# Local attention with a routed expert layer: the gather moved to the head of a block, two one-hot tiles and the clearing of columns moved to the next block

## The chip, the cores and the metric

The kernel runs on one core of a Trainium2 chip. The metric is the device time of one execution in microseconds (us); lower is better. A core has a matrix engine (PE), a vector engine (DVE), a scalar engine (ACT), a general engine (POOL, GpSimd) and DMA queues. Each engine takes its instructions in the order in which the program gives them, and they wait for one another by semaphores. SP is the engine that here only issues plain DMAs.

## The reference, cut to what matters

The input is 2 sequences of 2048 tokens with 256 features, in float32. The first half is attention in a local window with a residual and a layer norm. The second half, which the change touches, is an expert layer with one expert per token:

```python
x = L0_attn_x                                    # (2, 2048, 256)
x = _layernorm(x + attention(x))                 # eps 1e-5
# expert layer, 8 experts of 256 -> 1024, then a shared 1024 -> 256
idx = argmax(softmax(x @ Wr.T))
inter = sum_e (idx == e) * gelu(x @ W1[e] + b1[e])
y = layernorm(inter @ Wo + bo + x) * gamma + beta    # eps 1e-12
out = _layernorm(x + y)                          # eps 1e-5
```

## The kernel before

**Attention.** The first 32 tiles of 128 tokens go through attention in one long hand-ordered stretch. Each finished row is written to DRAM (`x1_d`), and the router's logits are computed on the way. Attention's last pieces end at about 328 us of the span.

**Blocks.** Tokens are then processed in blocks of 128 rows that belong to one expert. There are 25 full blocks (`NFULL`), 0 to 24, whose rows all belong to one expert, and later blocks for what is left over. Which tokens a block holds is a table of row numbers, `g_idx`. The table for blocks 0 to 8 (`g_idx_a`) is ready before the attention stretch ends, because it uses only the first 16 tiles of tokens. The table for blocks 9 to 24 (`g_idx_b`) is made in block 5 by `table(1)`: 32 matmuls on PE, one for each tile of tokens, that add into one result. Each takes as its weights a one-hot tile (`rows[t]`, `one_hots`, line 856) and as its moving operand a slice of `marks`, which DVE makes in steps of the task "others" (lines 928 to 940). Sixteen of the one-hot tiles are made for the last tokens in blocks 1 to 3.

**What a block does.** `block(b)` is a software pipeline over several blocks at once. Written in the order in which the program emits it:

- block b-1 is finished in steps by `finish_block`: DVE adds the residual to the second layer's result (line 264) and takes its statistics; POOL turns a variance into a reciprocal root by an add and a power (lines 255 and 256, `rs_b`); DVE scales twice (lines 267 and 269) and takes statistics again; POOL makes a second root (`rs_c`); DVE makes `res` (line 274), and POOL scatters it to the output by an indirect DMA (line 276, `out_dram`);
- POOL gathers the rows of block b+3 by an indirect DMA (line 150);
- PE runs the first layer of block b+1 (line 222, 32 matmuls), ACT applies the gelus (line 233);
- POOL makes the two residuals of block b+1 (lines 180 and 182, `xbo` and `xbe`);
- PE transposes the rows of block b+2 (line 188, `turn_in`), which a gather has brought one block before;
- PE runs the second layer of block b (line 242, 16 matmuls).

**Work beside.** The dictionary `beside` hangs small tasks into a block at three places. Place 0 comes after the first step of `finish_block`, place 1 after its statistics for the second root, and place 2 after the scatter and ahead of the second layer. The one-hots on POOL are at place 2, as are `table(1)` in block 5 and the clearing of columns of `late_gT` and `late_xT` (line 1506, shown by the profile as line 1471). The steps of "others" are at places 0 and 1 on DVE.

**Order.** All of this runs under a manual schedule: on each engine the instructions stand exactly as the program emits them, and semaphores are derived from the tiles that are read and written. Gathered rows have four buffers (`f6`), transposed rows and weights three, the second layer's results two banks.

Of the kernel before, what the change touches and what calls it, by code (L numbers as in the profile page):

```python
# [17 lines left out]
P = 128  # L18
# [15 lines left out]
def kernel(  # L34
# [16 lines left out]
    nc = tc.nc  # L51
# [9 lines left out]
    GB = 3  # L61
# [3 lines left out]
    NFULL = -((E * (P - 1) - B * T) // P)  # L65

    ND = NT - NFULL
# [66 lines left out]
    late = {}  # L134
# [5 lines left out]
    def of_block(tables, b, rows=slice(None)):  # L140
        n = 0 if b < NA else 1 if b < NFULL else 2
        at = b - (0, NA, NFULL)[n]
        return tables[n][rows, at : at + 1]

    def gather(b):
        if b < NFULL:
            xg = f6.tile([P, C], F32, tag="xg", name=f"xg_{b}")
        else:
            xg = late["d"].tile([P, C], F32, tag="xd", name=f"xd_{b}")
        nc.gpsimd.indirect_dma_start(  # L150
            out=xg,
            out_offset=None,
            in_=x1_d[0 : (SPLIT[EARLY] * P if b < NA else B * T), :],
            in_offset=bass.IndirectOffsetOnAxis(ap=of_block(g_idx, b), axis=0),
        )
        xgs[b] = xg
# [19 lines left out]
    def residuals(b):  # L176

        pool, n = (late["s"], "") if b < NFULL else (late["d"], "d")
        xbos[b] = pool.tile([P, C], F32, tag=f"xbo{n}", name=f"xbo_{b}")
        nc.gpsimd.tensor_tensor(xbos[b], xgs[b], bo_bc, ALU.add)  # L180
        xbes[b] = xgs[b] if n else pool.tile([P, C], F32, tag="xbe", name=f"xbe_{b}")
        nc.gpsimd.tensor_tensor(xbes[b], xgs[b], be_bc, ALU.add)

    def turn_in(b):
        px = turned(f"pg_{b}")
        px = px.rearrange("p a t -> p (a t)")
        for k in range(KC):
            nc.tensor.transpose(px[:, ts(k, P)], xgs[b][:, ts(k, P)], ident)
        if b < NFULL:
            xT = f3.tile([P, KC, P], F32, tag="xgT", name=f"xgT_{b}")  # L190
        else:
            xT = late["xT"][:, :, ts(b - NFULL, P)]
        xTs[b] = px, xT

    def keep_in(b):
        px, xT = xTs[b]
        nc.scalar.copy(xT, px[:, 0:C].rearrange("p (k t) -> p k t", k=KC))
# [10 lines left out]
    def first_layer(b, units):  # L208

        wb, xT = wbs[b], (picked[b][1] if b in picked else xTs[b][1])  # L210
        for f in units:
            h = f // (NF // 2)
            if f == 0:
                if b < NFULL:
                    gTs[b] = f2.tile([P, NF, P], F32, tag="gT", name=f"gT_{b}")
                banks_of[b] = 2 * (len(banks_of) % 2)
            if f % (NF // 2) == 0:
                phs[b, h] = ps_s.tile(
                    [P, 4, P], F32, tag=f"s{banks_of[b] + h}", name=f"ph_{b}_{h}"
                )  # L220
            for k in range(KC):
                nc.tensor.matmul(  # L222
                    phs[b, h][:, f % (NF // 2), :],
                    lhsT=wb[:, k, ts(f, P)], rhs=xT[:, k, :],
                    start=(k == 0), stop=(k == KC - 1),
                )

    def gelus(b, h):
        ph = phs.pop((b, h))

        gT = late["gT"][:, :, ds(picked[b][0], P)] if b in picked else gTs[b]
        for f in range(h * NF // 2, (h + 1) * NF // 2):
            nc.scalar.activation(  # L233
                gT[:, f, :], ph[:, f % (NF // 2), :], AF.Gelu,
                bias=bcs[b][:, f : f + 1], scale=1.0,
            )
# [11 lines left out]
    def stats(v, eps, name):  # L248

        st = fs.tile([P, 6], F32, tag=f"st{name[0]}", name=f"st_{name}")  # L250
        mv = fs.tile([P, 2], F32, tag=f"mv{name[0]}", name=f"mv_{name}")
        nc.vector.bn_stats(st, v)
        nc.vector.bn_aggr(mv, st)  # L253
        rs = fs.tile([P, 1], F32, tag=f"rs{name[0]}", name=f"rs_{name}")
        nc.gpsimd.tensor_tensor(rs, mv[:, 1:2], eps, ALU.add)  # L255
        nc.gpsimd.tensor_tensor(rs, rs, minus_half, ALU.pow)  # L256
        return mv, rs
# [3 lines left out]
    def finish_block(b, places=s_idx):  # L261

        y = late["3"].tile([P, C], F32, tag="y", name=f"y_{b}")
        nc.vector.tensor_tensor(y, pys.pop(b)[:, 0:C], xbos[b], ALU.add)  # L264
        mv, rs = stats(y, eps_ffn, f"b{b}")
        yield
        nc.vector.scalar_tensor_tensor(y, y, mv[:, 0:1], ga_bc, ALU.subtract, ALU.mult)
        yield
        nc.vector.scalar_tensor_tensor(y, y, rs, xbes[b], ALU.mult, ALU.add)
        yield  # L270
        mv, rs = stats(y, eps_block, f"c{b}")
        yield
        res = late["3"].tile([P, C], F32, tag="res", name=f"res_{b}")
        nc.vector.tensor_scalar(res, y, mv[:, 0:1], rs, ALU.subtract, ALU.mult)  # L274

        ins = nc.gpsimd.indirect_dma_start(  # L276
            out=of[:, :],
            out_offset=bass.IndirectOffsetOnAxis(ap=of_block(places, b), axis=0),
            in_=res,
            in_offset=None,  # L280
            bounds_check=B * T - 1,
            oob_is_err=False,
        )

        if places is s_idx:
            for other in written:
                tc.declare_no_dep(ins.ins, other.ins, reason="other rows")
            written.append(ins)
        yield


    with ExitStack() as att:
# [915 lines left out]
        for i in range(NT):  # L1208


            t, u, w, z = (n if n >= 0 else None for n in range(i, i - 4, -1))
# [127 lines left out]
        tiles = list(range(*lots[lot]))  # L1339
# [85 lines left out]
    def first_done(b):  # L1425

        at = line.index(b) + 3
        if at < len(line):
            load_weights(line[at])

    def block(b):

        last = finish_block(b - 1)
        next(last)
        for task in beside.get((b, 0), ()):
            task()
        if b + 3 < NFULL:
            gather(b + 3)
        if b + 1 < NFULL:
            first_layer(b + 1, range(NF // 2))  # L1440
            gelus(b + 1, 0)
            residuals(b + 1)
        next(last)
        next(last)
        next(last)
        for task in beside.get((b, 1), ()):
            task()
        if b + 1 < NFULL:
            first_layer(b + 1, range(NF // 2, NF))
            gelus(b + 1, 1)  # L1450
            first_done(b + 1)
        if b + 2 < NFULL:
            turn_in(b + 2)
            keep_in(b + 2)
        for n in firsts[b]:
            if n >= NFULL:
                first_layer(n, range(NF))
                gelus(n, 0)
                gelus(n, 1)
                first_done(n)  # L1460
        n = b - begin + 1 + NFULL
        if NFULL <= n < NFULL + ND:
            turn_in(n)
            keep_in(n)
            residuals(n)
        for m in firsts.get(b + 1, ()):
            if m >= NFULL:
                pick(m)
        next(last)
        for task in beside.get((b, 2), ()):  # L1470
            task()
        if begin - 2 <= b < begin - 2 + ND:
            gather(b - begin + 2 + NFULL)
        second_layer(b)
# [5 lines left out]
    beside = {  # L1480
        (1, 0): [partial(rest, ("hot", lot))],
        (1, 2): [partial(rank, lot)] + [partial(one_hots, nc.gpsimd, t) for t in tiles[:4:2]],
        (2, 0): [partial(rest, ("places", lot))],
        (2, 1): [partial(one_hots, nc.vector, t) for t in range(*lots[lot], 2)]
        + [partial(some, "others", 3)],
        (2, 2): [partial(one_hots, nc.gpsimd, t) for t in tiles[4:8:2]],
        (3, 0): [partial(some, "others", 6)],
        (3, 1): [partial(some, "others", 9)],
        (3, 2): [partial(one_hots, nc.gpsimd, t) for t in tiles[8::2]],
        (4, 0): [partial(some, "others", 3)],  # L1490
        (4, 1): [partial(rest, "others")],
        (5, 2): [partial(table, 1)],
        (14, 0): [partial(table, 2)],
    }
# [4 lines left out]
    for b in range(10, 14):  # L1499
        at = 8 * (b - 10)  # L1500
        beside[b, 0] = [partial(late_one_hots, nc.vector, at, at + 3)]
        beside[b, 1] = [partial(late_one_hots, nc.vector, at + 3, at + 8)]
    for b in range(4, 8):

        beside.setdefault((b, 2), []).append(
            partial(nc.gpsimd.memset, late["gT"][:, 2 * b - 8 : 2 * b - 6, (ND - GB) * P :], 0.0)
        )
    beside[8, 2] = [partial(nc.gpsimd.memset, late["xT"][:, :, ND * P :], 0.0)]

    def close(blocks, places):  # L1510

# [17 lines left out]
    for b in range(1, NFULL):  # L1529
        block(b)  # L1530
# [48 lines left out]
```

## Time and profile before

| | us |
|---|---|
| three runs | 584.72, 583.76, 584.75 |
| median | 584.72 |
| the profiled execution's own time | 584.71 |
| its span in the trace | 582.9 |
| time around the span | 1.8 |

| engine | busy us | share |
|---|---|---|
| PE | 555.4 | 95% |
| POOL | 409.1 | 70% |
| DVE | 397.2 | 68% |
| ACT | 302.0 | 52% |

The span is one execution as the trace shows it, from its first to its last instruction. Shares are means over stages with different limits, so for a change in one stage the timeline of that stage is what has to be read: for each engine the start of an instruction, its duration, what it is, and in brackets the idle time ahead of it with what ended that. Several of the same kind in a row are merged in one line (`x16`).

### The profile page before, as it was taken

To read this page: it belongs to the slowest core of one execution; us is meant where nothing else is said; L and a number is where in the kernel's file an instruction comes from. 1 tells how busy PE (TensorE), PEld (TensorE's weight loads), DVE (VectorE), ACT (ScalarE), POOL (GpSimd) and SP (SyncE) were. 2 spreads that over 40 slices of the span, in tenths; PEclk is the share of its full clock that TensorE was granted. 3 is DMA by queue.
4 is the path that set the end of the run, shared out by engine and by line. 5 is a ranking of instruction groups with operands and counts; after the bars stand their busy time and mean duration, and the time that the engine had idled before them with its cause. 6 is when DMAs were issued, how large, how long until landed. Compare 5 with 4: busy or idle time off the path is not lost. (4 is left out here: it accounts for less than half of the span.)

```text
span 582.9 us, 18515 instructions
## 1 busy us (share of the span) xinstructions
PE 555.4 (95%) x7311; PEld 452.4 (78%) x7312; DVE 397.2 (68%) x966; ACT 302.0 (52%) x1005; POOL 409.1 (70%) x603
## 2 busy tenths in 40 slices
PE   8999999999999999999898999999999999999991
PEld 5658667676776766766667899899999999999980
DVE  5559788887888788889977467887864242242483
ACT  2487675766758576675755433233334445545200
POOL 5359777676777877878983388888788767642484
PEclk9999999999999999999999999999999999999997
DMA  5301603012031120201343455555555766754010
GB/s 163 86 2 46 178 24 98 21 45 78 12 88 37 46 76 12 62 25 30 109 115 118 173 178 172 180 185 186 182 177 191 249 202 232 240 191 154 19 39 28
DMA packets 35605, 64.79 MB, mean 111 GB/s; under 512 B 8558, under 2 KB 23484, under 8 KB 35516
## 3 DMA queue, kind: packets, MB, share of 16 engines
q1 hardware_dynamic: 32444, 55.19, 30.2%
q0 software_dynamic: 3072, 8.39, 4.5%
q8 instruction: 59, 0.97, 0.7%
q14 instruction: 30, 0.25, 0.1%
HBM read 48.93 MB, written 8.39 MB: 98 GB/s over the span
## 5 line engine op out<-in xcount | busy, mean ns | idle before, releaser
L561 ACT ACTIVATE pr<-s,nm 128x128 f32<-128x128 f32 x512 | 142.1, 412 | 3.8 <-DVE nm L557 3.7
L573 POOL TENSOR_TENSOR fd<-pr 128x512 f32<-128x512 f32 x62 | 79.0, 1274 | 65.6 <-ACT pr L561 65.6
L233 ACT ACTIVATE gT<-ph,bc 128x128 f32<-128x128 f32 x200 | 57.2, 370 | 107.4 <-issue 60.4
L222 PEld LDWEIGHTS ph<-xgT,wb 128*128 128x128 f32 x800 | 93.5, 192 | 1.3
L222 PE MATMUL ph<-xgT,wb 128*128 128x128 f32 x800 | 94.4, 275 | 0.0
L242 PE MATMUL py<-wo_sb,gT 128*128 128x256 f32 x400 | 90.6, 380 | 0.0
L557 DVE TENSOR_REDUCE nm<-s 128x4 f32<-128x512 f32 x128 | 82.4, 683 | 5.9 <-PE s L545 5.5
L581 POOL TENSOR_TENSOR fd<-fd 128x512 f32<-128x512 f32 (+2 forms) x93 | 76.6, 824 | 7.3
L242 PEld LDWEIGHTS py<-wo_sb,gT 128*128 128x128 f32 x400 | 74.1, 190 | 9.0
L622 ACT COPY pT<-pt 128x512 f32<-128x512 f32 x64 | 38.3, 599 | 70.0 <-DVE nm L557 39.3
L616 PE MATMUL pt<-ident,pr 128*128 128x128 f32 x512 | 71.4, 280 | 1.8 <-ACT pT L622 0.6
L616 PEld LDWEIGHTS pt<-ident,pr 128*128 128x128 f32 x512 | 55.5, 141 | 18.2 <-issue 9.6
L426 PE MATMUL pj<-xT,wa 128*128 128x512 f32 x128 | 60.6, 595 | 0.8 <-issue 0.8
L264 DVE TENSOR_TENSOR y<-py,xbo 128x256 f32<-128x256 f32 x32 | 13.5, 422 | 52.9 <-PE py L242 52.8
L624 DVE COPY pT<-pt 128x512 f32<-128x512 f32 x64 | 43.8, 684 | 7.8 <-PE pt L616 7.8
L545 PEld LDWEIGHTS s<-k,q 32*64 32x64 f32 x2048 | 30.9, 130 | 15.0 <-issue 15.0
L222 PE MATMUL ph<-xpT,wb 128*128 128x128 f32 x352 | 40.8, 275 | 0.0
L222 PEld LDWEIGHTS ph<-xpT,wb 128*128 128x128 f32 x352 | 40.1, 192 | 0.1
L545 PE MATMUL s<-k,q 32*64 32x128 f32 x2048 | 38.6, 278 | 0.0
L426 PEld LDWEIGHTS pj<-xT,wa 128*128 128x128 f32 x128 | 21.7, 190 | 17.6 <-issue 15.5
L274 DVE TENSOR_SCALAR res<-y,mv_c,rs_c 128x256 f32<-128x256 f32 x32 | 15.9, 498 | 28.4 <-POOL rs_c L256 23.4
L255 POOL TENSOR_TENSOR rs_b<-mv_b,eps_ffn 128x1 f32<-128x1 f32 x32 | 9.3, 291 | 36.8 <-DVE mv_b L253 31.1
(235 smaller groups left out, 999.2 us busy)
## 6 DMA issues: line engine op xcount, KB each, us to landing
wb<-in_L_ffn_W_dram SPq DMA_DIRECT2D x33, 1024.0 KB
h<-v SPq DMA_DIRECT2D x24, 192.0 KB, 3.7
xt<-in_L_attn_x_dram SPq DMA_DIRECT2D x8, 512.0 KB, 4.0
x_d<-x SPq DMA_DIRECT2D x32, 128.0 KB, 1.8
wb<-in_L_ffn_W_dram SPq DMA_DIRECT2D x24, 128.0 KB, 2.1
h<-v SPq DMA_DIRECT2D x14, 96.0 KB, 2.7
wo_sb<-in_L_ffn_Wo_dram SPq DMA_DIRECT2D x1, 1024.0 KB
wa<-in_L_attn_W_attn_dram SPq DMA_DIRECT2D x3, 256.0 KB, 5.1
```

Source lines behind the costliest of these rows:

```text
L222: nc.tensor.matmul(phs[b, h][:, f % (NF // 2), :], lhsT=wb[:, k, ts(f, P)], rhs=xT[:, k, :], start=(k == 0), stop=(k == KC - 1),)
L233: nc.scalar.activation(gT[:, f, :], ph[:, f % (NF // 2), :], AF.Gelu, bias=bcs[b][:, f : f + 1], scale=1.0,)
L242: nc.tensor.matmul(py[:, 0:C], lhsT=gT[:, f, :], rhs=wo_sb[:, f, :], start=(f == 0), stop=(f == NF - 1),)
L426: nc.tensor.matmul(pm, lhsT=wa[:, k, ts(f, P)], rhs=axT[c][:, k, :], start=(k == 0), stop=(k == KC - 1),)
L545: nc.tensor.matmul(banks[i][r][a * CTX : (a + 1) * CTX, 2 * g + o, :], lhsT=qs[c][rows, g, o, t0 : t0 + CTX], rhs=ks[c][rows, g, t0 : t0 + P],
L557: nc.vector.tensor_reduce(maxes[i][:, r, :], banks[i][r], AX.X, ALU.max, negate=True)
L561: nc.scalar.activation(probs[i][:, r, x, :], banks[i][r][:, x, :], AF.Exp, bias=maxes[i][:, r, x : x + 1], scale=1.0,)
L573: nc.gpsimd.tensor_tensor(fd[:, 8 * pair : 8 * pair + 8, :], pr[:, two, :, 0:CTX].rearrange("p r x c -> p (r x) c"), pr[:, two, :, CTX:P]. ...
L581: nc.gpsimd.tensor_tensor(fd[:, :, 0:n], fd[:, :, 0:n], fd[:, :, n : 2 * n], ALU.add)
L616: nc.tensor.transpose(pt[:, x, :], probs[i][:, r, x, :], ident)
L622: nc.scalar.copy(pTs[i][:, r], pt)
L624: nc.vector.tensor_copy(pTs[i][:, r], pt)
```

## The change

Three moves in the order of the program; no arithmetic is changed.

1. In `block(b)`, the gather of block b+3 is emitted first of all, ahead of the first step of `finish_block(b - 1)`. Before, it came after that step and after the tasks at place 0.
2. Of the four one-hot tiles that POOL made at place 2 of block 3 (tokens' tiles 24 to 27), two (26 and 27) are made at place 2 of block 4.
3. The clearing of columns is moved by a block: `late_gT` from blocks 4 to 7 to blocks 5 to 8, `late_xT` from block 8 to block 9.

```diff
     def block(b):
 
+        if b + 3 < NFULL:
+            gather(b + 3)
         last = finish_block(b - 1)
         next(last)
         for task in beside.get((b, 0), ()):
             task()
-        if b + 3 < NFULL:
-            gather(b + 3)
         if b + 1 < NFULL:
             first_layer(b + 1, range(NF // 2))
...
-        (3, 2): [partial(one_hots, nc.gpsimd, t) for t in tiles[8::2]],
+        (3, 2): [partial(one_hots, nc.gpsimd, t) for t in tiles[8:10:2]],
         (4, 0): [partial(some, "others", 3)],
         (4, 1): [partial(rest, "others")],
+        (4, 2): [partial(one_hots, nc.gpsimd, t) for t in tiles[10::2]],
         (5, 2): [partial(table, 1)],
...
-    for b in range(4, 8):
+    for b in range(5, 9):
 
         beside.setdefault((b, 2), []).append(
-            partial(nc.gpsimd.memset, late["gT"][:, 2 * b - 8 : 2 * b - 6, (ND - GB) * P :], 0.0)
+            partial(nc.gpsimd.memset, late["gT"][:, 2 * b - 10 : 2 * b - 8, (ND - GB) * P :], 0.0)
         )
-    beside[8, 2] = [partial(nc.gpsimd.memset, late["xT"][:, :, ND * P :], 0.0)]
+    beside[9, 2] = [partial(nc.gpsimd.memset, late["xT"][:, :, ND * P :], 0.0)]
```

## The prediction

> **What bounds the kernel now.** I read PE's timeline from the start of the block stage first, because PE has the largest busy share (95%).
>
> ```profile
> 353.44 3.73 PE L222 MATMUL ph<-xgT,wb 128*128 128x128 f32 x32
> 357.01 0.38 PE L188 MATMUL pg<-ident,xg 128*128 128x128 f32 x2
> 357.23 3.62 PE L242 MATMUL py<-wo_sb,gT 128*128 128x256 f32 x16
> 360.68 3.73 PE L222 MATMUL ph<-xgT,wb 128*128 128x128 f32 x32
> 365.30 0.41 PE L188 MATMUL pg<-ident,xg 128*128 128x128 f32 x2 [0.88 <-DMA xg<-x_d,g_idx_a]
> 365.54 0.95 PE L951 MATMUL p_tok<-marks,row 128*128 128x32 bf16 x32
> 366.35 3.70 PE L242 MATMUL py<-wo_sb,gT 128*128 128x256 f32 x16
> 369.88 3.73 PE L222 MATMUL ph<-xgT,wb 128*128 128x128 f32 x32
> ```
>
> A block takes PE 7.24 us (353.44 to 360.68), back to back. Block 5 is the exception: its transposes (L188) come 4.62 us after the first layer's start, not 3.57 as in block 4. PE waits 1.05 us for the gather of block 7. After that PE is full again, so any time that PE loses or wins here reaches the end of the span. Two smaller holes of the same kind follow: first layers start 7.36 us apart around 380 and 7.50 around 395, 0.11 and 0.26 too long.
>
> Next I read why that gather was late, in POOL's timeline for blocks 3 and 4.
>
> ```profile
> 357.38 1.04 POOL L276 DMA_INDIRECT out_dram<-res,g_idx_a  x1 [1.14 <-DVE res L274]
> 358.46 2.56 POOL L856 TENSOR_SCALAR row<-col,lows 128x128 bf16<-128x128 f32 x4
> 361.00 0.18 POOL L255 TENSOR_TENSOR rs_b<-mv_b,eps_ffn 128x1 f32<-128x1 f32 x1
> 361.26 0.57 POOL L256 TENSOR_TENSOR rs_b<-rs_b,minus_half 128x1 f32<-128x1 f32 x1
> 362.02 1.31 POOL L150 DMA_INDIRECT xg<-x_d,g_idx_a  x1 [0.19 <-issue]
> 363.37 0.81 POOL L180 TENSOR_TENSOR xbo<-xg,bo_bc 128x256 f32<-128x256 f32 x1
> 364.14 0.89 POOL L182 TENSOR_TENSOR xbe<-xg,be_bc 128x256 f32<-128x256 f32 x1
> 365.00 0.23 POOL L255 TENSOR_TENSOR rs_c<-mv_c,eps_block 128x1 f32<-128x1 f32 x1
> 365.31 0.60 POOL L256 TENSOR_TENSOR rs_c<-rs_c,minus_half 128x1 f32<-128x1 f32 x1
> 366.65 1.04 POOL L276 DMA_INDIRECT out_dram<-res,g_idx_a  x1 [0.74 <-DVE res L274]
> ```
>
> POOL's gathers start 9.48, 9.06 and 9.40 us apart in blocks 1 to 4 (334.08, 343.56, 352.62, 362.02): it is over 7.24, so POOL falls behind PE. The gather of 362.02 frees PE at 365.30, 3.28 us after its start. POOL is also idle 1.14 us ahead of the scatter, for DVE's `res`; so I read DVE's turn in the same loop.
>
> ```profile
> 353.96 0.79 DVE L1011 TENSOR_TENSOR base<-first_of,taken 128x8 f32<-128x8 f32 x1
> 356.68 0.41 DVE L274 TENSOR_SCALAR res<-y,mv_c,rs_c 128x256 f32<-128x256 f32 x1
> 361.87 0.49 DVE L269 SCALAR_TENSOR_TENSOR y<-y,rs_b,xbe 128x256 f32<-128x256 f32 x1 [1.89 <-POOL rs_b L256]
> 365.95 0.41 DVE L274 TENSOR_SCALAR res<-y,mv_c,rs_c 128x256 f32<-128x256 f32 x1 [0.28 <-POOL rs_c L256]
> ```
>
> So there is a ring: POOL's `rs_b` frees DVE's L269; L269, statistics and the tasks at place 1 lead to `res`; `res` frees the scatter; then come the one-hots, and then `rs_b` of the next block. From L269 to `res` DVE takes 4.21 us in block 3 (352.47 to 356.68), 3.86 in block 2, 4.08 in block 4. The gather and the residuals stand beside this DVE time, so the gather's 1.31 us costs the ring nothing now.
>
> **The change part by part.** *The gather goes ahead of `rs_b`.* In block 1 it falls into POOL's idle 5.53 us ahead of 333.03 and is free: the residuals start 1.3 us earlier, and `res` follows `rs_c` about 0.93 us earlier. From block 2 on it stands in the ring: 0.18 gap + 1.31 + 0.04 = 1.53 us ahead of `rs_b`, on which L269 waits, then everything behind L269 on DVE, then the scatter. It is the wait that this change adds.
>
> *What DVE does then.* In before the place-1 tasks run beside `xbo` and `xbe`, and tiny ones are slow there: L1011 took 0.79 us on 128x8 beside `xbo`, L1047 0.17 on the same shape with POOL on a single-column operation. The Trainium skill (GPSIMD Engine Reference, section 1, Specifications) says that POOL shares SBUF interfaces with DVE, and that DVE instructions with two SBUF inputs are among those that contend. This trace agrees, and the rule speaks for a smaller loss: with the gather gone from between, `xbo` and `xbe` start at L269 and end at about L269 + 1.4, just after the tasks begin (L269 + 1.08). Without contention block 3's tasks would take about 2.0 us for 3.2, but L269 itself would suffer (0.76 for 0.48 where it met the gather's end and `xbo` at 431 us). By the unchanged rows D, from L269 to `res`, is 3.86, 4.21 and 3.75 (4.08 without 0.28 of waiting) in blocks 2, 3, 4; without contention about 3.3 each. I take 3.45, 3.50, 3.45, nearer to the freed case, as POOL does only single-column work beside most tasks.
>
> *The ring, worked out.* L269 comes 0.87 us after `rs_b`; the scatter 0.70 after `res`; 1.08 later POOL is free; one-hots are 0.645 each (2.58 for four).
> - Block 1: POOL ends at 342.53 - 0.93 = 341.60.
> - Block 2: `rs_b` 343.13, L269 344.00, `res` 347.45, scatter 348.15, end 348.15 + 1.08 + 2.58 = 351.81 (before 351.60).
> - Block 3: `rs_b` 353.34, L269 354.21, `res` 357.71, scatter 358.41, end with two one-hots 360.78.
> - Block 4: gather of block 7 at 360.96 (before 362.02), lands by the same 3.28 at 364.24; PE wants it at 364.25. The 1.05 us hole goes. Then `rs_b` 362.31, L269 363.18, `res` 366.63, scatter 367.33, and only then the two moved one-hots, done at 367.33 + 1.08 + 1.29 = 369.70.
>
> *The moved one-hots have a reader.* `table(1)` in block 5 reads `rows[26]` and `rows[27]`; PE reaches it at about 364.5. In before these tiles were done at 361.0 and hidden; now PE, in order, waits for 369.70. Some six matmuls of the table's 32 remain (0.95 us for 32): 0.2. The second layer starts at 369.9; before at 366.35. PE loses 3.55 us. What is behind it, second layer and first layer of block 7, waits with it.
>
> *The clearing.* Four memsets of 0.98 and one of 0.34 leave blocks 4 to 8 and enter 5 to 9. Block 4 is 0.98 lighter, which is already in the sum (none after its scatter); the columns are first read past 436 us, so there is no reader to be late for.
>
> *After block 5.* The late PE gives gathers slack: gather 8 starts at 369.88, lands some 4.15 later (376.70 to 380.79 and 391.22 to 395.53 in before say 4.1 to 4.3), and is wanted at 369.9 + 3.46 + 3.57 = 376.9: 2.9 us of slack. The holes of 0.11 and 0.26 go: -0.37. But the ring with a memset is 1.53 + 0.87 + D + 0.70 + 1.06 + 0.98 = 5.14 + D; with D reduced as above to 2.75, 3.1, 2.85, 3.1 in blocks 5 to 8 (unchanged rows 3.16, 3.75, 3.16, 3.34) it loses 0.64 + 0.99 + 0.74 + 0.99 = 3.36 against PE's 7.25: about 0.45 more than the slack, a hole at the transposes of block 12 near 400 us. Block 9 has the small memset and 2.2 of DVE; blocks 10 to 13 with no memset are at 7.0; no more is lost. From 16 on PE has 11 us per block and POOL catches up.
>
> *DMA and queues.* The same gathers, scatters and loads are issued. SP's queue has no step moved. On POOL's own queue the gather is now right behind the scatter (about 1 us after its end, 2 before); if it landed 0.5 us later, slack takes it in blocks 5 to 7.
>
> *The clock.* PE's idle stretch in block 5 is about 5 us in all. The trace has the price of a cold PE at its start: 16 transposes took 3.67 us, 229 ns each, where 32 matmuls of that size now take 3.73, 0.12 us each. The Trainium skill (TensorE: Matmul & The Clock Gate, section "What's actually happening") puts the fall to half rate after an idle window of about 3.4 us, and as long to recover. By the rows of before (PEclk 9 through holes to 1.24 us) I add nothing; by the rule it would be an estimated +1.7 us. I take nothing: PE is busy with the table's first 16 matmuls, waits for `marks` (to about 366.3), does 10 more, and waits again for 3.3 us, so no stretch quite fills a window. It stays in the upper range.
>
> Sum: 3.55 - 0.37 + 0.45 = +3.6 on the profiled execution's 584.71 (582.9 span and 1.8 around it; the median 584.72 is the same): **588.3 us**.
>
> **The rivals.** *Contention stays (slower still).* With D unchanged the same ring gives one-hots at 371.1, second layer 371.3, so +4.95, and holes of some 1.5 us near 395 and 403: +6.1, 590.8. For it: POOL's `xbo` still meets two-input DVE work. Against: tasks are clear of it.
>
> *Only the one-hots count (no change).* If the gather did not delay `rs_b`, block 4's L269 would come at 361.87 - 1.29 = 360.58, `res` 364.4, one-hots 367.5, second layer 367.7: +1.35 - 0.37 = +1.0, 585.7. Against it: POOL's next instruction starts 0.04 us after every gather's end.
>
> *The gather was the only thing in the way (faster).* Mechanism: PE's 1.05 us hole at the transposes in block 5 goes, with 0.37 later, and nothing replaces it: 583.3. It decides at the table: the one-hots must be done by about 365.1, so the scatter of block 4 has to be out at 362.7, some 3.9 us earlier than the 366.65 of before. Nothing in the change takes this much from POOL and DVE ahead of it.
>
> **How the numbers follow.** My forecast, a table that waits 3 to 5 us, has 0.70; contention kept, or a cold clock on top, 0.20; only the one-hots 0.05; faster 0.05. The forecast's own ends are the freed D (+2.4) and the middle of both D (+4.1) with a hole or two: 586.6 to 590. The range 586.4 to 590.7 leaves out the two last cases and half of the second. A change of 0.2%, 1.2 us, is about what can be told from none: faster 0.05, same 0.05, slower 0.90.
>
> **What would show it.** In PE's timeline: the transposes of block 5 at 364.3 without a wait; the table's matmuls split, the rest after POOL's one-hots at 368.5 to 371; the second layer at 369 to 371. In POOL's: gather, `rs_b`, residuals in this order, DVE's L269 of blocks 3 and 4 1.3 to 2.4 us later than before. Wrong would be: a table that runs at 364.5 to 366 in one piece; L269 no later; or matmuls of the first layer after it at twice their duration (the clock).

## The result and the profile after

| | us |
|---|---|
| before, median of 4 runs | 584.27 (583.76 to 584.75) |
| after, median of 4 runs | 588.66 (588.41 to 589.87) |
| ratio | 1.0081, 95% interval 1.0069 to 1.0094 |
| span of the profiled execution, before and after | 582.9, 586.7 |
| forecast | 588.3, range 586.4 to 590.7 |

The change makes the kernel 4.4 us slower, clear of noise. Everything is lost in one place, block 5. PE's timeline after the change, the part that answers to the one shown of before (start, duration, what, idle time before and its end):

```profile
360.38 3.73 PE L222 MATMUL ph<-xgT,wb 128*128 128x128 f32 x32
363.95 0.38 PE L188 MATMUL pg<-ident,xg 128*128 128x128 f32 x2
364.17 0.56 PE L951 MATMUL p_tok<-marks,row 128*128 128x32 bf16 x16
365.38 0.40 PE L951 MATMUL p_tok<-marks,row 128*128 128x32 bf16 x10 [0.65 <-DVE marks L940]
368.21 0.19 PE L951 MATMUL p_tok<-marks,row 128*128 128x32 bf16 x1 [2.43 <-POOL row L856]
368.80 0.32 PE L951 MATMUL p_tok<-marks,row 128*128 128x32 bf16 x5 [0.40 <-POOL row L856]
368.96 5.19 PE L242 MATMUL py<-wo_sb,gT 128*128 128x256 f32 x16
373.98 3.73 PE L222 MATMUL ph<-xgT,wb 128*128 128x128 f32 x32
```

The transposes (L188) no longer wait for the gather: they come 3.57 us after the first layer's start, as in block 4. The table (L951) now waits three times: for DVE's marks (0.65 us), and for each of the two moved one-hots (2.43 and 0.40). The second layer behind it takes 5.19 us where it took 3.70. From one first layer to the next, block 5 takes 13.60 us (360.38 to 373.98) against 9.20 before: +4.40. The holes of 0.11 and 0.26 us that before had near 380 and 395 are gone (-0.37). That is +4.03, and the block stage began 0.30 us earlier in this execution, so PE ends 3.73 later; the spans differ by 3.8.

Why the table waits is in POOL's timeline of blocks 3 and 4 after the change:

```profile
358.09 1.04 POOL L276 DMA_INDIRECT out_dram<-res,g_idx_a  x1 [1.55 <-DVE res L274]
359.18 1.32 POOL L856 TENSOR_SCALAR row<-col,lows 128x128 bf16<-128x128 f32 x2
360.67 1.06 POOL L150 DMA_INDIRECT xg<-x_d,g_idx_a  x1 [0.17 <-PE py L242]
361.76 0.20 POOL L255 TENSOR_TENSOR rs_b<-mv_b,eps_ffn 128x1 f32<-128x1 f32 x1
...
362.60 0.72 POOL L180 TENSOR_TENSOR xbo<-xg,bo_bc 128x256 f32<-128x256 f32 x1
...
366.42 1.05 POOL L276 DMA_INDIRECT out_dram<-res,g_idx_a  x1 [0.96 <-DVE res L274]
367.53 1.22 POOL L856 TENSOR_SCALAR row<-col,lows 128x128 bf16<-128x128 f32 x2
```

The gather of block 7 starts at 360.67, not 362.02, and that is what removed PE's hole. But the two one-hots stand behind block 4's scatter, which stands behind DVE's `res`, and run at 367.5 to 368.8; PE was at the table at 364.2.

DVE in the same stretch, the other half of the ring:

```profile
354.01 0.96 DVE L269 SCALAR_TENSOR_TENSOR y<-y,rs_b,xbe 128x256 f32<-128x256 f32 x1 [3.20 <-POOL rs_b L256]
355.73 0.20 DVE L1011 TENSOR_TENSOR base<-first_of,taken 128x8 f32<-128x8 f32 x1
357.39 0.41 DVE L274 TENSOR_SCALAR res<-y,mv_c,rs_c 128x256 f32<-128x256 f32 x1
362.65 0.96 DVE L269 SCALAR_TENSOR_TENSOR y<-y,rs_b,xbe 128x256 f32<-128x256 f32 x1 [2.11 <-POOL rs_b L256]
365.72 0.41 DVE L274 TENSOR_SCALAR res<-y,mv_c,rs_c 128x256 f32<-128x256 f32 x1
```

L269 waits longer for `rs_b` than before (3.20 us in block 3), as the gather is now ahead of `rs_b`. It also takes twice as long, 0.96 for 0.48 us, since POOL's `xbo` and `xbe` now run beside it; the tasks behind it have become short (L1011 0.20 for 0.79).

The clock, by stretches of PE's time in the changed kernel (columns: stretch, its length, busy time of PE, PEld, DVE, ACT and POOL with counts, granted clock, DMA share, GB/s):

```profile
364.00:366.00 2.00, 1.12 (x29) 0.93 (x27) 1.86 (x9) 1.41 (x5) 1.22 (x3) 1.00 0.43 33
366.00:369.00 3.00, 0.39 (x7) 0.30 (x7) 2.75 (x9) 0.00 (x0) 2.36 (x4) 0.93 0.97 373
369.00:371.00 2.00, 2.00 (x10) 1.64 (x7) 0.10 (x1) 0.00 (x0) 1.90 (x4) 0.50 0.17 41
371.00:372.50 1.50, 1.50 (x7) 1.22 (x6) 1.43 (x4) 0.00 (x0) 1.43 (x2) 0.67 0.09 33
372.50:374.00 1.50, 1.50 (x9) 1.32 (x8) 1.23 (x10) 0.00 (x0) 0.74 (x2) 1.00 0.00 0
```

Read in finer stretches of the same view, PE was granted half its clock from 368.57 to 371.98, 3.41 us that begin in the last short wait and lie almost wholly in the second layer. So the wait is paid twice: as idle time, and in the matmuls after it. Below, *cold* stands for half clock and *warm* for the full one.

### The profile page after: what moved, and what is told of

Read it like the earlier page. It is cut to its first block, busy times and chain, and to the rows that moved or that the text cites. A ratio compares the mean times of both kernels' runs of the same rounds, so it can differ in the third digit from the quotient of the medians.

```text
span 586.7 us, 18516 instructions
## 1 busy us (share of the span) xinstructions
PE 556.6 (95%) x7311; PEld 453.5 (77%) x7312; DVE 392.2 (67%) x966; ACT 301.9 (51%) x1005; POOL 407.0 (69%) x603
## 5 line engine op out<-in xcount | busy, mean ns | idle before, releaser
L242 PE MATMUL py<-wo_sb,gT 128*128 128x256 f32 x400 | 92.1, 384 | 0.0
L269 DVE SCALAR_TENSOR_TENSOR y<-y,rs_b,xbe 128x256 f32<-128x256 f32 x25 | 22.5, 899 | 31.6 <-POOL rs_b L256 31.4
L667 PE MATMUL py<-wpj,av 128*128 128x256 f32 x128 | 34.0, 388 | 1.0 <-ACT x1T L710 0.4
```

Of the source, the lines that this page charges most:

```text
L242: nc.tensor.matmul(py[:, 0:C], lhsT=gT[:, f, :], rhs=wo_sb[:, f, :], start=(f == 0), stop=(f == NF - 1),)
```

## The experiments

The theory is this: the early gather mends PE's hole but lengthens the ring of POOL and DVE; the two moved one-hots have a reader on PE that comes first; and the wait costs clock on top. The rivals: the gather's move is free, or the one-hots alone account for everything.

**Gather alone.** Only the first move is made.

```diff
     def block(b):
+        if b + 3 < NFULL:
+            gather(b + 3)
         last = finish_block(b - 1)
         next(last)
...
-        if b + 3 < NFULL:
-            gather(b + 3)
```

> Only the gather is moved to the head of the block; the one-hots and the clearing stay where they were before. My theory (the gather stands in the ring POOL rs_b, DVE L269 to res, POOL scatter): L269 of blocks 3 and 4 later than before as in the changed kernel, the gather of block 7 starts at about 362 because all four one-hots are ahead of it, so PE keeps a hole of about 1.3 us at the transposes of block 5; the table then waits for DVE's marks until about 366.6 but not for POOL; no cold matmuls. Second layer of block 5 some 1 us later than before, and a few tenths more from later holes: about 585.6, +1.3 us. Rival (the early gather is free and only the moved one-hots cost time): the hole of 1.05 us shrinks, 583.3 to 584.3.

Measured: 587.42 us against 584.71 of before in the same series, ratio 1.0045 (1.0032 to 1.0059). The gather's move is no gain by itself: the rival falls. Block 5 went as worked out, +0.94 us (10.14 for 9.20), with a gather at 362.18, hardly other than before, and a wait for DVE's marks. But 1.8 us came in two places that I had not expected. PE's timeline of this kernel in blocks 5 and 14:

```profile
365.21 0.41 PE L188 MATMUL pg<-ident,xg 128*128 128x128 f32 x2 [0.79 <-DMA xg<-x_d,g_idx_a]
366.88 0.55 PE L951 MATMUL p_tok<-marks,row 128*128 128x32 bf16 x16 [0.87 <-DVE marks L940]
...
428.89 0.83 PE L951 MATMUL p_tok<-marks,late_row 128*128 128x14 bf16 x27
430.26 0.96 PE L951 MATMUL p_tok<-marks,late_row 128*128 128x14 bf16 x5 [0.54 <-DVE late_row L862]
```

The second table, in block 14, waits for the last five one-hots that DVE makes behind L269 in block 13; from the first layer ahead of this table to the one behind it 9.49 us pass, 8.05 before. As I read the timelines, DVE is late since the ring is slower than PE through blocks 5 to 8 (gathers 7.34 to 7.94 us apart, where PE takes 7.24). The other hole is in block 15, in its transposes of the leftover rows: 7.80 us to the next first layer, 7.47 before. In the changed kernel PE is itself 4 us late by then, and neither hole shows.

**All but the gather.** One-hots and clearing are moved, the gather is not.

```diff
     def block(b):
-        if b + 3 < NFULL:
-            gather(b + 3)
         last = finish_block(b - 1)
         next(last)
...
+        if b + 3 < NFULL:
+            gather(b + 3)
```

> The one-hots and the clearing are moved as in the change, the gather stays behind rs_b. My theory: the hole at the transposes of block 5 goes, as the gather of block 7 starts 1.3 us earlier; L269 of block 4 at about 360.6, res 364.4, scatter 365.1, the two moved one-hots done at 367.4, so the table waits on POOL some 2.4 us and the second layer of block 5 starts 1.2 us later than before; later holes (0.37 us) gone: +0.9 us, 585.1, with a warm clock; with a cold second layer as in the changed kernel up to 586.6. Rival (the gather's move costs nothing, all of the loss is the moved one-hots): the same 588.6 as the changed kernel.

Measured: 587.36, ratio 1.0043 (1.0029 to 1.0056), +2.65 us. PE's timeline in block 5:

```profile
364.19 0.81 PE L951 MATMUL p_tok<-marks,row 128*128 128x32 bf16 x26
366.97 0.19 PE L951 MATMUL p_tok<-marks,row 128*128 128x32 bf16 x1 [1.97 <-POOL row L856]
367.55 0.29 PE L951 MATMUL p_tok<-marks,row 128*128 128x32 bf16 x5 [0.39 <-POOL row L856]
367.68 5.39 PE L242 MATMUL py<-wo_sb,gT 128*128 128x256 f32 x16
```

The second layer starts 1.3 us later than before (1.2 expected), and then runs cold although the long gap is under 2 us: 5.39 for 3.70 us. Block 5 takes 12.51 us for 9.20, of which 1.62 is the wait and 1.69 the clock; the mended holes (0.37) and a block stage that began 0.28 earlier in this execution bring that to the 2.65. The rival (all of the changed kernel's loss) falls too. The two parts, +2.7 and +2.65, make +4.4 together and not 5.4, as the late PE hides the gather's holes in blocks 14 and 15.

**One-hots early in block 4.** The whole change, with the two one-hots behind `rs_b`.

```diff
-        (4, 0): [partial(some, "others", 3)],
+        (4, 0): [partial(some, "others", 3)]
+        + [partial(one_hots, nc.gpsimd, t) for t in tiles[10::2]],
...
-        (4, 2): [partial(one_hots, nc.gpsimd, t) for t in tiles[10::2]],
```

> The whole change, but the two moved one-hots come in block 4 right behind rs_b and ahead of the residuals, not behind the scatter. My theory: they are done at about 364, the table waits only for DVE's marks (to about 365.5), the second layer of block 5 starts about 365.8, 0.3 us earlier than before, matmuls stay at full clock; the ring with the memset (7.4 us a block, PE 7.25) makes small holes in blocks 6 to 10 of about 0.7 us in all where before had 0.37: 584.3, no change against before, 4.3 us under the changed kernel. Rival (the loss is the gather's delay of the ring, the one-hots only mark it): the time stays within 1.5 us of the changed kernel, 587 to 588.6.

Measured: 586.14, ratio 1.0024 (1.0015 to 1.0033), +1.43 where I expected none; but nearly 3 us under the changed kernel's loss, which settles that the place of these two tiles makes most of it. The miss is in two terms. The residuals, pushed back, now met the marks on DVE, whose first operation took 0.95 us, not 0.39; PE's table waited for them until 365.87:

```profile
362.54 0.61 DVE L269 SCALAR_TENSOR_TENSOR y<-y,rs_b,xbe 128x256 f32<-128x256 f32 x1 [2.11 <-POOL rs_b L256]
363.75 0.95 DVE L928 TENSOR_TENSOR same<-label,at 128x256 f32<-128x256 f32 x1
364.73 0.83 DVE L935 TENSOR_TENSOR marks<-same,tile 128x256 bf16<-128x256 f32 x1
```

And block 14's table had the hole of "Gather alone" again, 8.93 us for 8.05, with 0.26 in block 15.

**A filled wait.** The whole change with 28 transposes of the identity ahead of the table, whose result nobody reads.

```diff
+    def fill(count):
+        pf = turned("fill")
+        for _ in range(count):
+            nc.tensor.transpose(pf[:, 0, :], ident, ident)
...
-        (5, 2): [partial(table, 1)],
+        (5, 2): [partial(fill, 28), partial(table, 1)],
```

> The whole change with 28 extra transposes of the identity on PE ahead of the table in block 5, which nobody reads; they fill some 3.1 us in which PE would wait for the one-hots. My theory (the wait makes the clock fall, and the next second layer pays 1.56 us for it): the one-hots are done at the same time, the second layer of block 5 starts within 0.2 us of the changed kernel's, but takes 3.6 us and not 5.2: 587.1, 1.6 us under the changed kernel. Rival (the slow 16 matmuls have another cause, such as late weights or gelus): no change, 588.6.

Measured: 587.62, +2.91 against before in its series, where the change has +4.39: 1.5 us back by adding work.

```profile
364.40 3.22 PE L1484 MATMUL fill<-ident 128*128 128x128 f32 x28
367.46 0.80 PE L951 MATMUL p_tok<-marks,row 128*128 128x32 bf16 x26
368.56 0.19 PE L951 MATMUL p_tok<-marks,row 128*128 128x32 bf16 x1 [0.29 <-POOL row L856]
369.40 0.29 PE L951 MATMUL p_tok<-marks,row 128*128 128x32 bf16 x5 [0.65 <-POOL row L856]
369.54 3.70 PE L242 MATMUL py<-wo_sb,gT 128*128 128x256 f32 x16
```

The second layer is back at 3.70 us. It starts 8.92 us after block 5's first layer (8.58 in the changed kernel), behind the same one-hots, so the slow matmuls came from idle PE time and from nothing in the data. The mean granted clock was 0.991 to 0.993 in all five executions, as in 14 of the 15 of before in that series; the changed kernel's four have 0.986 to 0.989.

**How long a wait may be.** 18 and 8 transposes in the same place, one execution each.

> The changed kernel with 18 extra transposes (read by nobody) ahead of the table in block 5, so that PE's wait for the first moved one-hot is about 1.3 us, in place of the 2.43 us of the changed kernel and the 0.29 us with 28 of them. My theory (it is one long gap that lets the clock fall; 1.1 us did not, 1.97 us did): the second layer of block 5 takes 3.6 to 3.7 us, clock 1.00 throughout. Rival (it is the busy share over some microseconds that counts, and tiny table matmuls hardly count): 5.2 us, as in the changed kernel.

> The same with 8 extra transposes: the wait for the first moved one-hot is about 2.3 us, but the idle time before it, for DVE's marks, is filled. My theory (one gap over some 2 us is enough): second layer of block 5 in 5.2 us, clock half for about 3.4 us. Rival (the sum of the idle time counts, and it is about 0.8 us less than in the changed kernel): 3.7 us.

Both expectations were wrong, and the wrong way round: with 18 (gaps of 1.31 and 0.66 us) the second layer took 5.39 us, total 588.51; with 8 (gaps of 0.40, 1.92 and 0.66) it took 3.70, total 586.95. The first execution with 18:

```profile
367.87 0.19 PE L951 MATMUL p_tok<-marks,row 128*128 128x32 bf16 x1 [1.31 <-POOL row L856]
368.72 0.29 PE L951 MATMUL p_tok<-marks,row 128*128 128x32 bf16 x5 [0.66 <-POOL row L856]
368.86 5.39 PE L242 MATMUL py<-wo_sb,gT 128*128 128x256 f32 x16
```

So neither a longest gap nor the sum of the idle time decides. The same two kernels over more executions:

> The kernel with 18 extra transposes once more, now timed over many executions. It showed a cold second layer after a gap of 1.31 us, where 8 transposes and a gap of 1.92 us left it warm. If the clock is decided by a window that runs on its own time, an execution falls in it by chance: times spread over two groups some 1.7 us apart, near 586.9 and 588.5. If the program alone decides (which matmuls fill the time), all executions are near 588.5 with the spread of the kernel before.

> The kernel with 8 extra transposes, timed over many executions. By a window on its own time: two groups, near 586.9 and 588.5. If the program alone decides: all near 586.9.

In the profiled executions of these the two had changed sides: 18 transposes, same gap, warm (first three lines); 8 transposes, a gap of 1.84, cold (last three).

```profile
368.28 0.19 PE L951 MATMUL p_tok<-marks,row 128*128 128x32 bf16 x1 [1.31 <-POOL row L856]
369.11 0.29 PE L951 MATMUL p_tok<-marks,row 128*128 128x32 bf16 x5 [0.65 <-POOL row L856]
369.25 3.70 PE L242 MATMUL py<-wo_sb,gT 128*128 128x256 f32 x16
...
369.02 0.19 PE L951 MATMUL p_tok<-marks,row 128*128 128x32 bf16 x1 [1.84 <-POOL row L856]
369.87 0.31 PE L951 MATMUL p_tok<-marks,row 128*128 128x32 bf16 x5 [0.66 <-POOL row L856]
370.02 6.62 PE L242 MATMUL py<-wo_sb,gT 128*128 128x256 f32 x16
```

Times were 587.97 to 590.07 with 18 (median 589.30, before 584.43), and 588.71 to 590.91 with 8 (median 589.46): no two clean groups near 586.9 and 588.5, and some slower than either, so this part of the expectation did not come. What is shown is that the same program at the same gap is warm in one execution and cold in another.

The traces also show what tells the two apart. The clock switched only at points that lie whole multiples of 3.413 us apart: in the changed kernel it fell at 368.57, rose at 371.98, and fell again, behind PE's last work, at 576.78, which is 60 times 3.413 us later. So the points in block 5 can be found from an execution's later switches even where the clock stayed up. PE's busy time in the emptiest stretch of block 5 between two such points, and the clock behind it:

| profiled execution | stretch, us | PE busy, us | clock behind it |
|---|---|---|---|
| changed kernel | 365.16 to 368.57 | 0.59 (17%) | half for 3.41 us |
| 8 transposes, second | 365.70 to 369.12 | 1.19 (35%) | half for 6.83 us |
| all but the gather | 365.19 to 368.60 | 1.24 (36%) | half for 3.41 us |
| 18 transposes, first | 366.30 to 369.71 | 1.44 (42%) | half for 3.41 us |
| 18 transposes, second | 367.32 to 370.73 | 1.81 (53%) | full |
| 8 transposes, first | 367.14 to 370.55 | 1.89 (55%) | full |
| gather alone | 364.77 to 368.19 | 2.11 (62%) | full |
| before | 362.73 to 366.15 | 2.54 (74%) | full |

In block 5 the clock fell after 42% or less and held after 53% or more (with the one-hots early after 68%, with 28 transposes after 72%). Where the points lie against PE's waits differs from one execution to the next, and with gaps like these that decides. It is no rule for every mix of matmuls: in the profile of the next experiment the clock fell at 35.87 us, in attention, after a stretch of 64%. With 8 transposes the second profile was cold for two stretches, the first of which holds the gap of 0.66 us; the second layer then took 6.46 us to the next first layer, 2.9 more than warm. With a block stage that began 1.1 us later than in the first, this makes its 590.91.

The Trainium skill (TensorE: Matmul & The Clock Gate, section "What's actually happening") gives the gate's window as 3413 ns and calls it free-running, not reset when a kernel starts; the switch points agree. It puts the fall to half rate after an idle window of about 3.4 us. Here gaps of 1.31 and 0.66 us, with the table's tiny matmuls around them, were enough when the points lay badly, and the measurement decides.

**Residuals later.** The whole change with `residuals(b + 1)` moved behind `rs_c`.

```diff
-            residuals(b + 1)
         next(last)
         next(last)
         next(last)
+        if b + 1 < NFULL:
+            residuals(b + 1)
```

> The whole change, with POOL's two residuals of a block moved behind rs_c, so that they no longer run beside DVE's L269 but beside the place-1 tasks. My theory (POOL and DVE slow each other whenever a POOL elementwise operation meets DVE work on two inputs, so contention moves and does not go): L269 takes 0.48 us and not 0.95, but the marks operations of block 4 take 0.6 to 0.9 us as in before, not 0.4; res of block 4 within 0.4 us of the changed kernel's 365.7, one-hots done at 368.5 to 369.2; 588.0 to 589.2. Rival (only L269 suffers, the tasks are slow in before for another reason): L269 0.48 and the tasks stay short, each block's ring is 0.47 us shorter, the one-hots are done 1.2 us earlier, 587.2 to 587.5.

Measured: 590.47, ratio 1.0108 (1.0093 to 1.0124): 1.7 us worse than the change, where I had at most 0.5. L269 was free again (0.48 us), and the marks stayed short as well (0.39, 0.42, 0.35), which the theory had not foreseen: POOL now idles 1.28 us for DVE's statistics and starts the residuals after the marks. They hit what came next, `res`:

```profile
363.97 0.48 DVE L269 SCALAR_TENSOR_TENSOR y<-y,rs_b,xbe 128x256 f32<-128x256 f32 x1 [2.12 <-POOL rs_b L256]
365.48 0.42 DVE L935 TENSOR_TENSOR marks<-same,tile 128x256 bf16<-128x256 f32 x1
366.48 0.58 DVE L1019 TENSOR_TENSOR taken<-taken,first_of 128x8 f32<-128x8 f32 x1
366.99 0.88 DVE L274 TENSOR_SCALAR res<-y,mv_c,rs_c 128x256 f32<-128x256 f32 x1
```

This execution runs 1.26 us behind the changed kernel's from before the first block (the cold stretch at 35.87 us lies there), so `res` at 366.99 is the 365.72 from there, no better, and it takes 0.88 us for 0.41. The moved one-hots come 0.47 us later for it, and block 5 takes 14.12 us, 0.52 more than in the changed kernel. The ring is not shortened by moving the contention: the second half of the theory stands, the rival falls. The rest of the 1.7 us is a new hole of 1.10 us in block 15, where PE waits for a leftover gather.

**Six one-hots in POOL's idle time.** Ahead of block 1 POOL is idle 5.5 us, and the columns that one-hots are made from are ready. Six of the twelve go there, and two each into blocks 1, 2 and 3; once on the kernel before, once on the changed kernel (with none in block 4).

```diff
+    for t in tiles[:6:2]:
+        one_hots(nc.gpsimd, t)
     for b in range(1, NFULL):
         block(b)
...
-        (1, 2): [partial(rank, lot)] + [partial(one_hots, nc.gpsimd, t) for t in tiles[:4:2]],
+        (1, 2): [partial(rank, lot)] + [partial(one_hots, nc.gpsimd, t) for t in tiles[6:8:2]],
...
-        (2, 2): [partial(one_hots, nc.gpsimd, t) for t in tiles[4:8:2]],
+        (2, 2): [partial(one_hots, nc.gpsimd, t) for t in tiles[8:10:2]],
...
-        (3, 2): [partial(one_hots, nc.gpsimd, t) for t in tiles[8::2]],
+        (3, 2): [partial(one_hots, nc.gpsimd, t) for t in tiles[10::2]],
```

> The kernel before with six of the twelve one-hots made ahead of block 1, in POOL's idle 5.5 us, and two each in blocks 1, 2 and 3; gather and clearing as before. My theory: POOL falls behind by 1.3 us less in each of blocks 1 to 3, so the gather of block 7 starts by 358.5, the transposes of block 5 do not wait, the table waits for nothing on POOL; holes later (0.37 us) go as well: 583.3, 1.4 us under before. Rival (PE's hole is bounded by something other than POOL's one-hots, or the early one-hots push rs_b of block 1 back): 584.7 or more.

> The changed kernel (gather first, clearing a block later) with the one-hots of the run named idle before: six ahead of block 1 and two each in blocks 1, 2 and 3, none in block 4. My theory (the gather in the ring costs about 1.1 us a block, and shows only where the ring with it is over PE's 7.25 us): no wait for one-hots and no cold matmuls, the transposes of block 5 on time, but rings of 7.4 to 7.6 us in blocks 4 to 8 use up the slack; about 583.5 to 584.5, at most as good as the run without the gather's move. Rival (the gather's move is a gain once the one-hots are out of the way): under 583.3, faster than the run without it.

Measured: 582.71 on the kernel before (ratio 0.9976, 0.9966 to 0.9985) and 582.76 on the changed one (0.9978, 0.9971 to 0.9986), both about 1.6 us faster than before and the best of all runs. In the first the six tiles took POOL 3.50 us in the idle stretch, and the gather of block 7 started at 357.28, 4.7 us earlier than before:

```profile
328.00 3.50 POOL L856 TENSOR_SCALAR row<-col,lows 128x128 bf16<-128x128 f32 x6 [0.81 <-PE pl L727]
...
357.28 1.31 POOL L150 DMA_INDIRECT xg<-x_d,g_idx_a  x1 [0.19 <-PE pg L188]
```

In both, PE has no wait left between 330 us and its last second layer; block 5 takes 8.13 us (before 9.20, after 13.60). The gather's place then makes no difference: with slack in hand, a ring slower than PE for four blocks does not catch up with it. I had expected the second to lose up to 1 us; by the medians it lost nothing. Three of its 17 executions, at 584.0 to 584.3, have a mean clock of 0.988, the others 0.991 to 0.993.

## Why the prediction was right, and where it was not

The forecast was +3.6 us on 584.71, and +4.39 on 584.27 was measured. That the total came so near (588.3 against 588.66) is in part luck, as errors in its terms cancelled. By its own division of cases, what came is the table's wait with a cold clock on top, which had 0.20 together with kept contention, and not the wait alone, which had 0.70.

- *The hole at block 5's transposes goes*: forecast to go, gone. The gather started at 360.67 (forecast 360.96).
- *The moved one-hots have a reader*: right, and the largest term. Forecast 3.55 us between before's and after's start of the second layer; by the two timelines it is 2.91 (8.58 us after block 5's first layer started, against 5.67). The terms inside were off both ways. The gather cost the ring 1.27 us and not 1.53, as it ran 1.06 to 1.08 us, not 1.31, with DVE waiting beside it. D, from L269 to `res`, was 3.16, 3.38 and 3.07 in blocks 2 to 4, where I took 3.45, 3.50 and 3.45. Against this, block 1's gain of 0.93 did not come: there L267 and L269 met the residuals (1.06 and 0.76 us), and `res` was only 0.1 earlier.
- *The contention rule of the Trainium skill* (GPSIMD Engine Reference, section 1, Specifications) decided D, and the trace sides with it: tasks clear of POOL's two-input work became short (L1011 0.20 us for 0.79), L269 beside it doubled (0.96 for 0.48). Nearer to the freed case was right; even that was too careful. DVE work with one tensor input was slow beside that POOL work as well, `res` in "Residuals later" (0.88 us for 0.41).
- *The clock* is the term that was mis-sized: I took nothing, the rule's estimate was +1.7, and it was +1.5. The failed step is "no stretch quite fills a window": the gaps (0.65, 2.43, 0.40) did not fill one, and the clock fell all the same, after a stretch in which PE was busy for 0.59 of 3.41 us. The prediction had named the sign, matmuls at twice their duration; the slow ones came in the second layer, while the first layer behind it took its usual 3.73 us.
- *The hole of 0.45 at block 12's transposes* did not come; with shorter D the ring ran at 7.4 to 7.6 us, not up to 8.2, and the slack held. The 0.37 of before's later holes went, as forecast.
- *Slips in the working*, on which nothing rests: block 4's D without its 0.28 of waiting is 3.80 and not 3.75; with D freed to 3.3 the sum gives +2.7 (3.55 - 0.50 - 0.37), not +2.4; and that PE was cold at the trace's start is not shown, as the view gives a granted clock of 1.00 there. L269 of block 4 came 0.78 us later than before, less than the 1.3 named as a sign; in block 3 it was 1.54.

So: -0.64 on the wait, +1.5 on the clock, -0.45 on the later hole, +0.4 together. The rivals with no change and with a gain failed where the text said: POOL is in order behind the gather, and the scatter came at 366.42, not at 362.7.

## What to carry to other kernels

Before a small task is put off, look up who reads it and when that reader is due: two tiles of 1.3 us together cost 3 us (the clock included), since their new place stood behind a chain of another engine. Moving a step ahead of a wait also puts it in front of whatever that wait releases. An engine that falls behind is better helped from its own idle time: putting six of the same twelve tiles at 328 us, 12 to 19 us earlier, gave 1.6 us.

## What the hardware showed beyond that

- Half a clock after short gaps: PE lost 1.5 to 1.7 us in 16 matmuls behind gaps of 1.3 to 3.3 us, and 2.9 where the clock stayed at half for two stretches of 3.41 us. The same program at the same gap was cold in one execution and warm in another (5.39 and 3.70 us). What told them apart in block 5 was PE's busy share in the stretch of 3.41 us ahead of a switch point: 42% or less was followed by half clock, 53% or more was not.
- DVE's scale with two tensor inputs took 0.48 us alone and 0.95 beside a POOL addition. The indirect gather's issue took 1.31 us on POOL in blocks 2 to 4 of before, with DVE at work beside it, and 1.06 to 1.08 in the changed kernel, with DVE waiting; but at 432.27 in the changed kernel it took 0.99 with DVE at work, so what sets its length stays open.
